# Layer-2 attention scores taken from h W by VectorE inside GraphSAGE's loop, V scaled by one VectorE operation, the projection's pools allotted later

## The chip, the cores and the metric

The kernel runs on one core of one Trainium2 chip. The metric is device time in microseconds (us), the median of several executions. The core has five engines that run side by side and each take their instructions in order: TensorE (PE, with its weight loads shown as PEld), VectorE (DVE), ScalarE (ACT), GpSimd (POOL, which here issues the gathers) and SyncE (SP, which issues the plain DMAs).

## The reference, cut to what matters

Four graph layers run one after another on 3327 nodes with 512 features, and one sparse adjacency matrix serves all of them. Each layer normalises its input, applies a rectifier and adds its result to the input. Layer 0 is graph attention with batch normalisation, layer 1 is GraphSAGE (a mean over the neighbours and two linear maps), and layers 2 and 3 are graph attention with 8 heads of 64 features. The change touches what layer 2's attention needs from its input:

```python
x = x + _L1_gnn_ref(h, adj, ...)
h = jnp.maximum(_layernorm(x, axis=-1), 0.0)
Wh = jnp.einsum('nd,hdo->hno', x, W)
f1 = jnp.einsum('hno,ho->hn', Wh, a1)
f2 = jnp.einsum('hno,ho->hn', Wh, a2)
e = leaky_relu(f1[:, :, None] + f2[:, None, :])
attention = softmax(where(adj > 0, e, NEG_INF))
h_prime = jnp.einsum('hnm,hmo->hno', attention, Wh)
```

The scores f1 and f2 are sums of h W times a1 or a2 over each head's 64 features. They can be had either from h times a narrow matrix (W times a, summed per head, 16 columns), or from h W itself, once that is there.

## The kernel before, in words

All data is fp32. The 3327 nodes are padded to 3328, that is 26 blocks (NB) of 128 rows. The kernel first turns the adjacency matrix into lists of neighbours (`lists`), then tests whether they fit, and runs `sparse`; a dense branch (`general`) exists for other graphs and does not run here. `sparse` goes through these stages in order: attention 0 (`attend`), batch normalisation and layer norm, GraphSAGE, attention 2, attention 3.

**The SAGE loop (from L1472 backwards).** The neighbours of a block lie in up to 37 chunks of 128 gathered rows in the first block and 10 or so in the last ones; there are 359 in all. `load` copies a chunk's mask to fp32 on ScalarE (z_mask, L1453) and gathers its rows of h from HBM through GpSimd (z_rows, L1115, 8 buffers of two chunks). TensorE adds each chunk into sage_acc (L1472). When a block has its last chunk, the generator `ending` takes it on in steps: ScalarE scales it by the degree (s_ag, L1411), TensorE transposes it (a_ps, L1415), ScalarE copies it (aT, L1417), TensorE multiplies by the neighbours' weight (n_ps, L1421), VectorE adds the node's own part y and then the old x (s_o, L1426 and L1427), SP stores it, and `proj.begin` hands the block to the next layer's projection.

**The projection of layer 2 (`Following`) runs inside this loop.** `norm` computes the layer norm's sums on ScalarE (ln_j, L777 and L779), the inverse root partly on VectorE (rs_h, rs_g, rs_y: L713, L715, L719), and the normalised rows ln_h on ScalarE (L788). `rest` then does, for each block: four transposes on TensorE (p_ps, L795); rectifier into hT on ScalarE (L798); the scores p_sd, four fp32 matmuls of hT with the 16 columns of WA (L803, eight records in the profile, since an fp32 matmul is recorded as two); three small ScalarE operations on them (L807, L808, L810); a clip on VectorE (L813); h W into p_wh, four matmuls of 512 columns (L816); exponentials (`halves`, L730 and L731); eight ScalarE operations that scale each head of p_wh into v_row (L820); the store of v_row to the table in HBM (L821); a transpose of the 16 halves (p_tr, L824), its copy r_row (L827) and its store (L829). The four PSUM tiles p_ps, p_sd, p_wh and p_tr take turns in two PSUM banks (pb=2).

**What sets the order.** Every group of chunks calls `tick`, which advances each pending `ending`, each `norm` and up to two `rest` generators by one step, so the generators' `yield`s say where the steps may fall. The loop stands under no written-out order: a scheduling layer that builds the program places the instructions on each engine's in-order queue by their dependences. In the attention stages, the order of TensorE, VectorE and ScalarE is written out by hand; there layer 3's projection runs beside attention 2 with the same class. Attention 2's first gathers need the whole table and so the last block's v_row.

**Memory.** Pools are stacked. The projection's pools (`following`, called with pb=2 before the batch normalisation) lie under those of SAGE, of the batch normalisation (fbn) and of the layer norm (fln), so its weight fWt (L749) can be loaded early. WA for all layers is computed in the first stage by `Products`, which also uses it for a test of range.

Of the kernel before, what the change touches and what calls it, by code (L numbers as in the profile page):

```python
# [23 lines left out]
F32 = mybir.dt.float32  # L24
# [3 lines left out]
I32 = mybir.dt.int32  # L28
# [3 lines left out]
AF = mybir.ActivationFunctionType  # L32
ALU = mybir.AluOpType
ET = mybir.EngineType
AX = mybir.AxisListType
# [3 lines left out]
P = 128  # L39
H = 8  # L40
F = 64
D = H * F
KC = D // P
# [7 lines left out]
GB = 64  # L51
# [5 lines left out]
ROW = H * (F + 1) + H  # L57
# [4 lines left out]
SMALL = 53.0  # L62
# [393 lines left out]
class Products:  # L456
# [4 lines left out]
    def __init__(self, tc, t, pool, wp):  # L461
        self.nc, self.t, self.wp = tc.nc, t, wp
        self.WA = []
        for l in range(3):
            WA = pool.tile([P, KC, 2 * H], F32, name=f"WA{l}")
            self.WA.append(WA)
        self.ok = pool.tile([1, 1], I32, name="ok")
# [234 lines left out]
def rsqrt(nc, pool, cs, v, scale=1.0, bufs=3):  # L702


    n = v.shape[1]
    y = pool.tile([P, n], F32, name="rs_y", tag=f"rs_y{n}", bufs=bufs)
    g = pool.tile([P, n], F32, name="rs_g", tag=f"rs_g{n}", bufs=bufs)
    nc.scalar.activation(g, v, AF.Ln, scale=scale, bias=cs["eps"])
    nc.scalar.activation(y, g, AF.Exp, scale=-0.5)

    def step():
        h = pool.tile([P, n], F32, name="rs_h", tag=f"rs_h{n}", bufs=bufs)
        nc.vector.tensor_scalar(h, v, -0.5 * scale, -0.5 * EPS, ALU.mult, ALU.add)  # L713
        if n == 1:
            nc.vector.tensor_scalar(g, y, y, h, ALU.mult, ALU.mult)  # L715
        else:
            nc.vector.tensor_tensor(g, y, y, ALU.mult)
            nc.vector.tensor_tensor(g, g, h, ALU.mult)
        nc.vector.scalar_tensor_tensor(y, g, 1.5, y, ALU.add, ALU.mult)  # L719
        return y  # L720

    return step


def halves(nc, pool, cs, sf):


    rf = pool.tile([P, H], F32, name="r_full", tag="r_full", bufs=2)
    rs = pool.tile([P, 2, H], F32, name="r_half", tag="r_half", bufs=2)
    nc.scalar.activation(rf, sf, AF.Exp, scale=0.8, bias=cs["down"])  # L730
    nc.scalar.copy(rs.bitcast(F32R)[:, 0, :], rf)  # L731

    def other():
        nc.vector.tensor_tensor(rs.bitcast(F32R)[:, 1, :], rf, rs[:, 0, :], ALU.subtract)
        return rs.rearrange("p t h -> p (t h)")

    return other


class Following:  # L740

    def __init__(self, tc, cs, N, wl, W, WA, table, r_dram, pool, psum, pb=1):
        self.__dict__.update(locals())
        nc = tc.nc
        self.NB = table.shape[0] // P
        self.Wt = pool.tile([P, KC, D], F32, name=f"fWt{wl}")
        nc.sync.dma_start(self.Wt, W.rearrange("(kc p) o -> p kc o", p=P))  # L749
        self.hs = pool.tile([P, self.NB, KC], F32, name=f"hs{wl}")  # L750
        self.early, self.ready = [], []
# [4 lines left out]
    def tick(self):  # L756
        for _ in range(min(2, len(self.ready))):
            while self.ready and next(self.ready[0]) is None:
                self.ready.pop(0)
        for g in list(self.early):  # L760
            hx = next(g)
            if hx is not None:
                self.early.remove(g)
                self.ready.append(self.rest(*hx))

    def drain(self):
        while self.early or self.ready:
# [4 lines left out]
    def norm(self, c, xt):  # L772
        nc, pp, cs = self.tc.nc, self.pool, self.cs

        junk = pp.tile([P, D], F32, name="ln_j", tag="ln_j", bufs=1)
        st = pp.tile([P, 4], F32, name="ln_s", tag="ln_s", bufs=3)
        nc.scalar.activation(junk, xt, AF.Identity, accum_out=st[:, 0:1])  # L777
        nc.scalar.mul(st[:, 1:2], st[:, 0:1], -1.0 / D)
        nc.scalar.activation(junk, xt, AF.Square, bias=st[:, 1:2], accum_out=st[:, 2:3])  # L779
        step = rsqrt(nc, pp, cs, st[:, 2:3], 1.0 / D)  # L780
        yield
        y = step()
        if c == self.NB - 1:
            nc.vector.tensor_tensor(y, y, cs["real"], ALU.mult)
        yield
        hx = pp.tile([P, D], F32, name="ln_h", tag="ln_h", bufs=3)
        nc.scalar.mul(st[:, 3:4], st[:, 1:2], y)
        nc.scalar.activation(hx, xt, AF.Identity, scale=y, bias=st[:, 3:4])  # L788
        yield c, hx

    def rest(self, c, hx):
        nc, pp, WA, wl = self.tc.nc, self.pool, self.WA, self.wl
# [294 lines left out]
def sparse(ctx: ExitStack, tc: tile.TileContext, t: dict, out: bass.AP, WA, ls, cs, idx, rdeg, first):  # L1087
# [5 lines left out]
    nc = tc.nc  # L1093
    N = out.shape[0]
# [5 lines left out]
    def used(c):  # L1100
        return min(P, N - c * P)
# [18 lines left out]
    def attend(layer, table, r_dram, finish, tick=lambda: None, home=None):  # L1120
# [11 lines left out]
        with tc.tile_pool(name=f"fatt{layer}", bufs=2) as ap, tc.tile_pool(  # L1132
# [48 lines left out]
            def later():  # L1181
                for e in list(ends):
                    if next(e, 0) == 0:
                        ends.remove(e)
                tick()
# [60 lines left out]
            while ends:  # L1246
                later()

    def following(lx, layer, wl, W, pb=1):

        table = dram.tile([NP, ROW], I32, name=f"table{layer}")
        r_dram = dram.tile([ls.G, 2, H, GB], F32, name=f"r_dram{layer}")
        pp = lx.enter_context(tc.tile_pool(name=f"fproj{layer}", bufs=1))
        pps = lx.enter_context(tc.tile_pool(name=f"fproj_ps{layer}", bufs=1, space=PSUM))
        return Following(tc, cs, N, wl, W, WA, table, r_dram, pp, pps, pb)

    def elu_into(xin, dst, then=lambda c, xt: None):
        def finish(c, hp, pool):
# [21 lines left out]
    with ExitStack() as mx:  # L1280
# [3 lines left out]
        bias = mid.tile([P, D], F32, name="sage_b")  # L1284
# [56 lines left out]
        Wx = mid.tile([P, 2, KC, D], F32, name="fWx")  # L1341
        nc.sync.dma_start(Wx, wx_dram.rearrange("k kc p o -> p k kc o"))

        proj = following(mx, 2, 1, t["L2_gnn_W"], 2)
        gp = mx.enter_context(tc.tile_pool(name="fsage", bufs=2))
        gps = mx.enter_context(tc.tile_pool(name="fsage_ps", bufs=2, space=PSUM))
        two = [P, 2, D]
        with tc.tile_pool(name="fbn", bufs=1) as bp:
            var_ps = gps.tile([P, D], F32, name="var_ps", tag="n_ps")
            for c in range(0, NB, 2):  # L1350
                d = bp.tile(two, F32, name="bn_d", tag="bn_d", bufs=2)
                nc.vector.tensor_tensor(d, y[:, c : c + 2, :], mean.unsqueeze(1).to_broadcast(two), ALU.subtract)
                nc.scalar.activation(d, d, AF.Square)
                for i in range(2):
                    k = used(c + i)
# [7 lines left out]
        with tc.tile_pool(name="fln", bufs=1) as bp:  # L1363
# [24 lines left out]
            def own(c):  # L1388
                tp = gps.tile([P, KC, P], F32, name="h_ps", tag="a_ps")
                for kc in range(KC):  # L1390
                    nc.tensor.transpose(tp[:, kc, :], y[:, c, kc * P : (kc + 1) * P], cs["ident"])
                hT = bp.tile([P, KC, P], F32, name="hT", tag="hT", bufs=2)
                nc.scalar.copy(hT, tp)  # L1393
                ps = gps.tile([P, D], F32, name="s_ps", tag="n_ps")
                for kc in range(KC):
                    nc.tensor.matmul(ps, hT[:, kc, :], Wx[:, 0, kc, :], start=(kc == 0), stop=(kc == KC - 1))  # L1396
                nc.vector.tensor_tensor(y[:, c, :], ps, bias, ALU.add)
# [6 lines left out]
            for i in range(2):  # L1404
                own(NB - 2 + i)

        ends = []

        def ending(b, acc):
# [51 lines left out]
        for i, (b, _, begins, stops) in enumerate(parts):  # L1461
            load(i + SAHEAD)
            if begins:
                acc = gps.tile([P, D], F32, name="sage_acc", tag="sage_acc")
            at = -1
            for r, u, k, m, z in loaded.pop(i):
                if r != at:
                    at = r
                    tick()
                g = b * PG + u  # L1470
                f, l = k == ls.first[g], k == ls.first[g] + CAPS[g] - 1
                nc.tensor.matmul(acc[u * GB : (u + 1) * GB, :], m, z, start=f, stop=l)  # L1472
            if stops:
                ends.append(ending(b, acc))
        while ends:
            tick()
# [3 lines left out]
    with ExitStack() as l3:  # L1480
        at2 = proj
        proj = following(l3, 3, 2, t["L3_gnn_W"])
        attend(2, at2.table, at2.r_dram, elu_into(x2, x3, proj.begin), proj.tick)
        proj.drain()
# [88 lines left out]
```

## Time and profile before

| What | us |
| --- | --- |
| Median of 3 runs (2575.82, 2585.0, 2585.8) | 2585.0 |
| The profiled execution, its own time | 2951.92 |
| Its span, first to last instruction | 2950.1 |
| Busy: TensorE matmuls / VectorE / ScalarE / GpSimd | 2161.4 / 1781.5 / 1115.7 / 1381.8 |
| Mean granted TensorE clock | 0.791 |

The profiled execution is 14% longer than the median, so times read from it are larger than those of a plain run. A stage is a window of the span. A row of a group reads: line, engine, operation, tile written and tiles read, shape and count, then busy time in us and mean duration of one in ns, then the idle time of the engine just before these instructions and what ended most of it. "issue" is time in which an engine waited for nothing that the profile shows. The ends of matmuls are modelled.

### The profile page before, as it was taken

The page shows a single profiled execution, that of the slowest core. Times are in us where ns is not written, and L with a number is a line of the kernel's source. Part 1 is how long each engine was busy: PE and PEld are TensorE (multiplying, and loading weights), DVE is VectorE, ACT ScalarE, POOL GpSimd, SP SyncE. Part 2 cuts the span into 40 slices and gives each one's busy share as a digit, 9 for nine tenths or more (in the row PEclk, how much of TensorE's full clock was granted, in tenths as well). Part 3 has the DMA queues.
Part 4 walks back from the last instruction along what each step waited for, and adds up shares of the span by engine and source line. Part 5 has one row for each costly group of instructions (what it writes and reads, how often), then busy time and mean ns, then how long its engine had stood idle before and what let it go on. Part 6 is the DMA issues. An engine that isn't in the chain of part 4 may idle for free.

```text
span 2950.1 us, 54237 instructions
## 1 busy us (share of the span) xinstructions
PE 2161.4 (73%) x21320; PEld 1372.2 (47%) x21320; DVE 1781.5 (60%) x2194; ACT 1115.7 (38%) x4044; POOL 1381.8 (47%) x1482
## 2 busy tenths in 40 slices
PE   4777577767775976888998567877777657767775
PEld 2444354555552422233333355655555345556564
DVE  7648587878786800011111377777776277888886
ACT  4543022333434412344455213555666501232333
POOL 1001365666550055665554365555444066666563
PEclk9778688977777997899999777777787766675765
DMA  7761577877662746666665466666565166667774
GB/s 309 282 251 46 174 235 233 252 214 209 201 203 82 246 145 187 189 207 212 198 196 183 133 184 186 200 198 188 178 178 166 45 192 190 193 200 198 201 205 131
DMA packets 188773, 562.09 MB, mean 191 GB/s; under 512 B 37732, under 2 KB 42272, under 8 KB 185182
## 3 DMA queue, kind: packets, MB, share of 16 engines
q0 software_dynamic: 115456, 404.86, 47.2%
q1 hardware_dynamic: 73054, 153.67, 14.7%
q8 instruction: 171, 2.80, 0.4%
q14 instruction: 92, 0.75, 0.1%
HBM read 498.74 MB, written 59.68 MB: 189 GB/s over the span
## 4 chain that ended last, share of the span: by engine, by line
PE 54%; issue 16%; ACT 9%; another core or an unknown queue 3%; DVE 3%; DMA 2%; POOL 1%; SPq 0%; DVEq 0%; ACTq 0%; POOLq 0%
PE facc L1237 28%; PE p_wh L816 7%; PE sage_acc L1472 5%; PE n_ps L1421 3%; PE r_bc L1148 2%; PE p_sd L803 2%; PE s_ps L1396 2%; ACT v_row L820 2%; ACT fhp L1175 1%; PE fwx_ps L1314 1%; PE bmean_ps L1324 1%; PE p_ps L795 1%; ACT hT L798 1%; DMA rows<-table,idx 1%
## 5 line engine op out<-in xcount | busy, mean ns | idle before, releaser
L1115 POOL DMA_INDIRECT rows<-table,idx x1077 | 1023.4, 950 | 873.2 <-PE facc L1237 361.7
L1237 PE MATMUL facc<-rows,wgt 128*64 128x65 f32 x17232 | 975.3, 268 | 412.7 <-issue 394.5
L1237 PEld LDWEIGHTS facc<-rows,wgt 128*64 128x64 f32 x17232 | 826.5, 176 | 628.7 <-issue 576.9
L1223 DVE TENSOR_TENSOR wgt<-mx,mask 128x1536 f32<-128x1536 f32 (+1 forms) x405 | 638.4, 1576 | 158.6 <-PE facc L1237 75.0
L1216 DVE TENSOR_TENSOR mx<-r_bc,rows 128x1536 f32<-128x1536 f32 (+1 forms) x405 | 639.6, 1579 | 144.7 <-PE facc L1237 65.9
L1115 POOL DMA_INDIRECT z_rows<-h_dram,idx x359 | 339.4, 945 | 387.0 <-ACT hT L1393 139.5
L1175 ACT ACTIVATE fhp<-sums,rd 64x64 f32<-64x64 f32 x832 | 219.8, 334 | 137.0 <-DVE rd L1169 71.8
L1472 PE MATMUL sage_acc<-z_rows,z_mask 128*64 128x512 f32 x718 | 225.2, 639 | 9.5 <-DMA z_rows<-h_dram,idx 6.2
L816 PE MATMUL p_wh<-fWt,hT 128*128 128x512 f32 x416 | 227.7, 695 | 1.4 <-ACT s_col L810 1.4
L1165 ACT COPY sums<-facc 128x260 f32<-128x260 f32 x156 | 57.7, 370 | 405.0 <-PE facc L1237 354.3
L813 DVE TENSOR_SCALAR s_col<-s_col 128x8 f32<-128x8 f32 x52 | 9.2, 177 | 306.0 <-issue 135.9
L1208 ACT ACTIVATE mask<-on 128x192 uint8<-128x192 uint16 (+1 forms) x135 | 46.5, 344 | 378.8 <-DVE on L1202 214.1
L816 PEld LDWEIGHTS p_wh<-fWt,hT 128*128 128x128 f32 x416 | 90.3, 228 | 109.8 <-issue 105.3
L820 ACT ACTIVATE v_row<-p_wh,v_row 128x64 f32<-128x64 f32 x416 | 90.4, 328 | 125.8 <-PE p_wh L816 99.3
L1426 DVE TENSOR_TENSOR s_o<-n_ps,bn_y 128x512 f32<-128x512 f32 x26 | 18.0, 691 | 192.2 <-issue 95.6
L1036 POOL DMA_DIRECT2D list_b<-shift x12 | 5.9, 503 | 273.4 <-DVE shift L990 273.4
L680 PE MATMUL wh_ps<-fWt,hT 128*128 128x512 f32 x208 | 128.9, 777 | 0.0
L803 PE MATMUL p_sd<-WA,hT 128*128 128x16 f32 x416 | 74.4, 303 | 70.3 <-ACT hT L798 46.2
L803 PEld LDWEIGHTS p_sd<-WA,hT 128*128 128x128 f32 x416 | 71.8, 246 | 103.9 <-ACT hT L798 59.6
L1175 ACT ACTIVATE bn_y<-sums,rd 64x64 f32<-64x64 f32 x416 | 109.5, 333 | 2.4 <-DVE rd L1169 0.5
L1421 PE MATMUL n_ps<-fWx,aT 128*128 128x512 f32 x208 | 106.1, 646 | 5.6 <-ACT aT L1417 5.5
L1148 PE MATMUL r_bc<-r_two,fones 2*128 2x512 f32 x156 | 95.3, 615 | 14.8 <-issue 8.1
(198 smaller groups left out, 2108.0 us busy)
## 6 DMA issues: line engine op xcount, KB each, us to landing
adj_i<-in_adj SPq DMA_DIRECT2D x26, 1664.0 KB
table<-v_row SPq DMA_DIRECT2D x78, 264.0 KB
rows<-table,idx POOLq DMA_INDIRECT x1077
fin_x<-fx SPq DMA_DIRECT2D x52, 256.0 KB
ln_x<-in_x SPq DMA_DIRECT2D x26, 256.0 KB
bn_x<-in_x SPq DMA_DIRECT2D x13, 512.0 KB
fx<-bn_x SPq DMA_DIRECT2D x13, 512.0 KB
fsage_x<-fx SPq DMA_DIRECT2D x26, 256.0 KB
```

The source lines that it names most:

```text
L680: nc.tensor.matmul(wh, hT[:, kc, :], self.Wt[:, kc, :], start=(kc == 0), stop=(kc == KC - 1))
L803: nc.tensor.matmul(sd[:, : 2 * H], hT[:, kc, :], WA[wl][:, kc, :], start=(kc == 0), stop=(kc == KC - 1))
L816: nc.tensor.matmul(wh, hT[:, kc, :], self.Wt[:, kc, :], start=(kc == 0), stop=(kc == KC - 1))
L820: nc.scalar.mul(V[:, h, 0:F], wh[:, h * F : (h + 1) * F], V[:, h, F : F + 1])
L1115: nc.gpsimd.indirect_dma_start(out=dst, out_offset=None, in_=src[:, :], in_offset=bass.IndirectOffsetOnAxis(ap=idx[:, k : k + 1], axis=0))
L1148: nc.tensor.matmul(rb, ones[0:2, :].bitcast(F32R), rrs.pop(g).bitcast(F32R), start=True, stop=True)
L1175: nc.scalar.mul(hp[o0 : o0 + GB, h * F : (h + 1) * F], sm[mine, q, 0:F], rd[mine, q, :])
L1216: nc.vector.tensor_tensor(mx[:, :n], rbs[g].unsqueeze(1).to_broadcast(full), gt[:, :n, H * (F + 1) : ROW].unsqueeze(3).to_broadcast(full), ...
L1223: nc.vector.tensor_tensor(wt[:, :n], mx[:, :n], mk.unsqueeze(2).to_broadcast(full), ALU.mult)
L1237: nc.tensor.matmul(accs[g][v * GB : (v + 1) * GB, q * (F + 1) : (q + 1) * (F + 1)], wt[:, k, h, :], gt[:, k, h * (F + 1) : (h + 1) * (F + 1)],
L1421: nc.tensor.matmul(ps, aT[:, kc, :], Wx[:, 1, kc, :], start=(kc == 0), stop=(kc == KC - 1))
L1472: nc.tensor.matmul(acc[u * GB : (u + 1) * GB, :], m, z, start=f, stop=l)
```

## The change

`Following` takes an optional pair `ab` of score vectors. Layer 2 gives (a1, a2); layer 3 gives none and keeps `rest`. With `ab`, both vectors are loaded into SBUF, repeated over the partitions, and the new generator `rest_by_rows` takes the place of `rest`. It computes h W first, multiplies it on VectorE by both vectors at once (128 x 1024 products) and sums each head's 64 products (16 sums). The matmuls with WA and the ScalarE copy of the scores go. The eight ScalarE operations that scale V become one VectorE operation. The generator has one `yield` less. The call of `following` for layer 2 moves from before the batch normalisation to after the layer norm's pool is closed, so that its tiles take memory that fbn and fln used.

```diff
-    def __init__(self, tc, cs, N, wl, W, WA, table, r_dram, pool, psum, pb=1):
+    def __init__(self, tc, cs, N, wl, W, WA, table, r_dram, pool, psum, pb=1, ab=None):
         self.__dict__.update(locals())
         nc = tc.nc
+        if ab is not None:
+            self.ab = pool.tile([P, 2, D], F32, name=f"ab{wl}")
+            for k, a in enumerate(ab):
+                nc.sync.dma_start(self.ab[:, k, :], a.partition_broadcast(P))
...
-                self.ready.append(self.rest(*hx))
+                self.ready.append((self.rest if self.ab is None else self.rest_by_rows)(*hx))
...
+    def rest_by_rows(self, c, hx):
+        nc, pp = self.tc.nc, self.pool
+        tp = self.psum.tile([P, KC, P], F32, name="p_ps", tag="p_ps", bufs=self.pb)
+        for kc in range(KC):
+            nc.tensor.transpose(tp[:, kc, :], hx[:, kc * P : (kc + 1) * P], self.cs["ident"])
+        hT = pp.tile([P, KC, P], F32, name="hT", tag="hT", bufs=2)
+        for kc in range(KC):
+            nc.scalar.activation(hT[:, kc, :], tp[:, kc, :], AF.Relu, accum_out=self.hs[:, c, kc : kc + 1])
+        yield True
+        self.mean(c, hT)
+        wh = self.psum.tile([P, D], F32, name="p_wh", tag="p_ps", bufs=self.pb)
+        for kc in range(KC):
+            nc.tensor.matmul(wh, hT[:, kc, :], self.Wt[:, kc, :], start=(kc == 0), stop=(kc == KC - 1))
+        yield True
+        pr = pp.tile([P, 2, D], F32, name="sd_pr", tag="sd_pr", bufs=1)
+        nc.vector.tensor_tensor(pr, wh.unsqueeze(1).to_broadcast([P, 2, D]), self.ab, ALU.mult)
+        sd = pp.tile([P, 2 * H], F32, name="sd_col", tag="sd_col", bufs=2)
+        nc.vector.tensor_reduce(sd, pr.rearrange("p k (h f) -> p (k h) f", f=F), AX.X, ALU.add)
+
+        sf = pp.tile([P, H], F32, name="s_col", tag="s_col", bufs=2)
+        nc.vector.tensor_scalar(sf, sd[:, :H], -SMALL, SMALL, ALU.max, ALU.min)
+        row = pp.tile([P, ROW], F32, name="v_row", tag="v_row", bufs=2)
+        V = row[:, : H * (F + 1)].rearrange("p (h f) -> p h f", f=F + 1)
+        d = sd[:, H : 2 * H]
+        nc.scalar.activation(V[:, :, F : F + 1], d.rearrange("p (h o) -> p h o", o=1), AF.Exp)
+        nc.scalar.activation(row[:, H * (F + 1) :], d, AF.Exp, scale=-0.8, bias=self.cs["down"])
+        rs = halves(nc, pp, self.cs, sf)
+        yield True
+        nc.vector.tensor_tensor(
+            V[:, :, 0:F], wh.rearrange("p (h f) -> p h f", f=F), V[:, :, F : F + 1].to_broadcast([P, H, F]), ALU.mult
+        )
+        nc.sync.dma_start(self.table[c * P : (c + 1) * P, :ROW], row.bitcast(I32))
+        rs = rs()
+        yield True
+        tr = self.psum.tile([2 * H, P], F32, name="p_tr", tag="p_ps", bufs=self.pb)
+        nc.tensor.transpose(tr, rs, self.cs["ident"])
+        rr = pp.tile([2 * H, P], F32, name="r_row", tag="r_row", bufs=2)
+        nc.scalar.copy(rr, tr)
...
+        yield None
...
-    def following(lx, layer, wl, W, pb=1):
+    def following(lx, layer, wl, W, pb=1, ab=None):
...
-        return Following(tc, cs, N, wl, W, WA, table, r_dram, pp, pps, pb)
+        return Following(tc, cs, N, wl, W, WA, table, r_dram, pp, pps, pb, ab)
...
-        proj = following(mx, 2, 1, t["L2_gnn_W"], 2)
         gp = mx.enter_context(tc.tile_pool(name="fsage", bufs=2))
...
                 own(NB - 2 + i)
 
+        proj = following(mx, 2, 1, t["L2_gnn_W"], 2, (t["L2_gnn_a1"], t["L2_gnn_a2"]))
         ends = []
```

More of the change, by code (lines that the diff above doesn't have):

```diff
@@ L789, in norm @@
         yield c, hx
+    def rest_by_rows(self, c, hx):
[35 more added lines that the diff above has]
+        nc.scalar.copy(rr, tr)
+        n = P // GB
+        nc.sync.dma_start(
+            self.r_dram[c * n : (c + 1) * n, :, :, :].rearrange("g t h i -> (t h) g i"),
+            rr.rearrange("h (g i) -> h g i", i=GB),
+        )
+        yield None
```

## The prediction, made before the changed kernel was run

> **What bounds the kernel now.** I read the windows by stage first, since a mean over the whole span mixes stages with different limits. These are GraphSAGE (SAGE below) and its neighbours, then the SAGE loop in three pieces. The columns are length, then busy time (instructions) of PE, PEld, DVE, ACT and POOL, granted clock, DMA share, GB/s.
>
> ```profile
> 1032.00:1665.00 633.00, 517.44 (x1667) 204.28 (x1666) 65.40 (x193) 251.00 (x1054) 337.05 (x357) 0.91 0.59 182
> 1665.00:2355.00 690.00, 507.67 (x6340) 368.08 (x6340) 483.48 (x507) 339.49 (x1326) 336.87 (x356) 0.76 0.59 171
> ...
> 1120.00:1400.00 280.00, 223.94 (x729) 86.41 (x730) 26.77 (x80) 106.67 (x457) 170.29 (x181) 0.90 0.66 202
> 1400.00:1610.00 210.00, 193.19 (x652) 77.78 (x650) 26.81 (x82) 107.97 (x461) 117.21 (x124) 0.96 0.65 199
> 1610.00:1665.00 55.00, 38.29 (x114) 17.14 (x110) 6.29 (x24) 25.20 (x108) 4.23 (x5) 0.81 0.23 76
> ```
>
> In SAGE, TensorE is busy 517 of 633 us and VectorE 65. In the late blocks (1400 to 1610) TensorE reaches 92%. The next stage, attention 2, keeps VectorE busy 483 of 690 us; the new operations don't go there. Next I asked for the chain of waits over 1120 to 1660, to see which work of the projection sets the pace:
>
> ```profile
> by line: PE sage_acc L1472 21.9%; PE n_ps L1421 14.6%; PE p_wh L816 12.6%; another core or an unknown queue 8.7%; issue 7.4%; ACT v_row L820 5.0%; PE p_sd L803 4.8%; PE a_ps L1415 2.6%; PE p_ps L795 2.5%; DMA z_rows<-h_dram,idx 2.4%; ACT ln
> ```
>
> Both steps that the change takes away are on it: the score matmuls (4.8%) and ScalarE's scaling of V (5.0%). The groups of 1120 to 1645 give durations:
>
> ```profile
> L1472 PE MATMUL sage_acc<-z_rows,z_mask 128*64 128x512 f32 x636 | 197.7, 641 | 3.5 <-issue 1.9 <-DMA z_rows<-h_dram,idx 1.5
> ...
> L820 ACT ACTIVATE v_row<-p_wh,v_row 128x64 f32<-128x64 f32 x200 | 43.3, 326 | 30.5 <-PE sage_acc L1472 19.5 <-remote 7.0 <-PE p_wh L816 4.0
> ...
> L803 PE MATMUL p_sd<-WA,hT 128*128 128x16 f32 x200 | 29.5, 265 | 12.1 <-issue 12.1
> L803 PEld LDWEIGHTS p_sd<-WA,hT 128*128 128x128 f32 x200 | 29.2, 203 | 39.8 <-issue 33.1 <-ACT aT L1417 3.2 <-ACT hT L798 3.2
> ...
> L1426 DVE TENSOR_TENSOR s_o<-n_ps,bn_y 128x512 f32<-128x512 f32 x26 | 18.0, 691 | 192.2 <-issue 95.6 <-PE n_ps L1421 55.6 <-PE sage_acc L1472 10.6
> ```
>
> The z gathers could be a second bound. POOL's waits from 1020 to 1670:
>
> ```profile
> POOL z_rows L1115 <- PE sage_acc L1472: 92.8, 34, 8.3
> ...
> POOL z_rows L1115 <- PE p_tr L824: 46.4, 10, 7.3
> ```
>
> POOL waits 139 us for TensorE to give buffers back: TensorE is late, not the gathers. The timeline of TensorE at 1560 shows how ScalarE holds it up:
>
> ```profile
> 1560.38 1.94 PE L1472 MATMUL sage_acc<-z_rows,z_mask 128*64 128x512 f32 x8
> 1565.34 0.44 PE L795 MATMUL p_ps<-fident,ln_h 128*128 128x128 f32 x2 [3.02 <-ACT r_row L827]
> ```
>
> TensorE stands still for 3.02 us until ScalarE, which has just run its eight V scalings (1.73 us), delivers ln_h and r_row.
>
> [...] 128x1024 from PSUM (mx) took 1232 ns, 128x512 (s_o) 691.
>
> **The change, part by part.** All sums are in microseconds of the profiled execution (2951.92, span 2950.1), which is 14% above the median of 2585.0; I convert at the end.
>
> *Score matmuls removed.* 26 blocks of 8 records. Busy time 29.5 in 25 blocks, 1.18 each, so 31 for 26; on the chain 4.8% of 540 is 26. I take -26; bounds -31 and -10 (if much of it only fills waits).
>
> *Eight V scalings and the s_col copy removed from ScalarE.* 8 x 0.33 recorded, 1.74 per block because they overlap: 45 us of ScalarE, and 26 copies of 0.17 add 4. On the chain L820 has 5.0% of 540, 27. Not all comes back: behind it z_mask, s_ag, aT and the layer norm stay on the same in-order engine. What is late next is TensorE itself or the norm's chain. I take two thirds, -18; bounds -27 and 0.
>
> *VectorE's three new operations.* The product over 2 x 512 from PSUM: 1.23 (the mx row). The sum over 1024 elements to 16: a 512-element reduce (L481) took 0.69; a further 512 at the 0.53 to 0.54 by which 1024 exceeds 512 above gives 1.22. V scaled in one operation: 0.69 (L636 does just this in the first projection). Together 3.14, times 26: 82 on an engine idle for 568 of 633. As work it is hidden. As latency it isn't by itself: p_tr (and so the PSUM bank) needs product, sum, clip (0.17), exp (0.30), cast (0.20) and subtraction (0.17) after the last p_wh matmul, 3.3, some 3.9 with hand-overs of 0.1. In the built program's order, most late blocks have eight sage_acc matmuls and three transposes between p_wh and p_tr: 8 x 0.485 plus 0.4 is 4.3; most middle blocks have n_ps (3.43) and one to three sage_acc instead. The cover is thin. Behind the waiting product on VectorE stand rs_g and rs_y of the next norm, for which ln_h and then p_ps wait. I take +5; bounds 0 and +82, if every block waits in full.
>
> *Projection allotted later.* Its DMAs (fWt, 1 MB) leave SP's place at 900 us, ahead of bn_x, where it was issued 40 us before the next load; nothing waited for it. They now stand behind the last h_dram store and wait for the layer norm's pool, free when the last s_ps product has been added, about 1075; with the two 256 KB broadcasts 1.5 MB, 5 us at the 309 GB/s that the fastest slice of the profile page shows, beside the first gathers. SP's next instruction is the store of s_o at 1125, and p_wh first needs the weights at 1132, so the wait itself holds up nothing. I take +2; bounds 0 and +8 if the first gathers queue behind it. POOL's own order is unchanged. Cover lost: if it landed after 1132, each late us costs one.
>
> *End of the stage.* For the last block, product, sum, exps (0.4) and V (0.69) with hand-overs, about 3.8, replace score matmuls (1.0) and scalings (1.74) ahead of the table's store, on which attention 2's gathers wait: +1; bounds 0 and +2.
>
> *Unchanged.* WA of layer 2 is still computed for the range test; layer 3 keeps the old rest.
>
> Sum: -26 - 18 + 5 + 2 + 1 = -36, 1.2%; scaled by 2585/2952 (0.876), -31.5, so about 2553.
>
> **Rivals.**
> *The wait moves to VectorE (slower).* Product, sum and scaling stand between p_wh and p_tr in every block, with two PSUM banks for p_ps, p_wh and p_tr, and TensorE in order behind p_tr. For it: the cover is only 0.4 us too long, and rs_g stands behind the product. Against: VectorE is otherwise nearly idle, and p_sd no longer takes a bank. Price: 26 x 3.14 = 82, less the 53 removed at most, plus 29; times 0.876, +25: 2610. It decides once TensorE waits over 2.0 us per block (53/26).
> *Gathers take over (no change).* In the first 14 blocks (up to 37 gathers at 1.25 us) TensorE's freed time would become waiting for z_rows; for it is 2.4% of the chain in z_rows, against it POOL's 139 us. Then 12 blocks of 26 gain: -36 x 12/26 = -17, times 0.876: 2570; with a thin VectorE wait besides, 2580.
> *ScalarE was the true pacer (larger gain).* Both chain terms in full, -53, [...]: -65, times 0.876: 2528.
> *It doesn't do what it says.* In the built program p_sd is gone from SAGE alone and nothing before it moves but the weight load; I give this no chance of its own.
>
> **How the numbers follow.** Forecast 0.57 (2540 to 2570), larger gain 0.08, no change 0.17, slower 0.18. About 0.5% (13 us) is what a measurement of this kernel tells from no change: faster is 0.66 (forecast, larger gain, a little of the no-change case), same 0.16, slower 0.18. The range 2522 to 2600 takes in the larger gain and the no-change case, and half-paid VectorE waits, and leaves out most of the slower one.
>
> **What would show it.** SAGE, 1032 to 1665, should take about 597 us in the profile after, TensorE's busy time there down by some 30, ScalarE's by 45 or more, VectorE's up by 82. The new product should show 1.2 us. Right if POOL's waits for sage_acc shrink; wrong if p_tr or p_ps waits for VectorE or for r_half more than 2 us per block, or if idle time before sage_acc goes to z_rows.

## The result and the profile after

| | us |
| --- | --- |
| Before, median of 4 runs | 2583.64 |
| After, median of 4 runs (2553.76 to 2558.84) | 2557.27 |
| Ratio after to before | 0.9919, 95% interval 0.9901 to 0.9937 |
| After, profiled execution: its own time / span / clock | 2553.76 / 2551.8 / 0.851 |

The change made the kernel faster by 0.8% (0.6% to 1.0%), which is 21 us (16 to 26); the two medians stand 26 us apart. The profile after has a span close to its median, whereas the profile of before that the prediction worked from had 2950. A second profile of the kernel before, `e0_before_again`, has a span of 2576.2, and it is the one that the profile after is compared with below.

The stages by window, from the first sage_acc matmul to the first gather of attention 2, and from there to the end; columns as in the prediction. First before (`e0_before_again`):

```profile
941.00:1470.00 529.00, 495.32 (x1666) 195.28 (x1664) 66.20 (x194) 254.73 (x1054) 334.10 (x353) 0.98 0.71 216
1470.00:2576.00 1106.00, 741.94 (x12138) 596.90 (x12138) 942.95 (x881) 498.24 (x1846) 685.57 (x718) 0.77 0.71 209
```

Then the changed kernel:

```profile
937.00:1448.00 511.00, 460.62 (x1463) 168.24 (x1461) 141.92 (x272) 209.30 (x820) 335.64 (x355) 0.98 0.74 229
1448.00:2552.00 1104.00, 729.23 (x12136) 584.41 (x12136) 943.23 (x881) 498.18 (x1846) 686.10 (x718) 0.79 0.71 208
```

The gain lies in SAGE: 529 became 511, and the stages around it differ by 2 to 4 us. TensorE's busy time in SAGE fell by 34.7, ScalarE's by 45.4, and VectorE's rose by 75.7. TensorE lost 35 us of work and the stage became only 18 shorter, so half of what was freed turned into idle time. Two stretches of the loop fare differently: from the first p_ps transpose of block 0 to that of block 10 (blocks count from 0), and from there to that of block 25. Before:

```profile
1021.10:1228.10 207.00, 192.81 (x656) 73.26 (x655) 23.23 (x70) 100.54 (x417) 156.68 (x166) 0.99 0.80 247
1228.10:1453.80 225.70, 222.75 (x784) 92.16 (x783) 34.61 (x106) 134.91 (x571) 129.15 (x137) 1.00 0.70 216
```

After:

```profile
1017.50:1227.60 210.10, 189.96 (x590) 64.41 (x590) 53.87 (x100) 84.27 (x331) 159.22 (x168) 0.99 0.80 247
1227.60:1432.20 204.60, 191.92 (x651) 74.86 (x649) 76.29 (x151) 107.18 (x431) 127.54 (x135) 0.99 0.75 235
```

The whole gain lies in the later stretch, where TensorE was busy for 99% of the time before: 226 became 205. In the first ten blocks nothing was gained (207 and 210). The chain of waits over the loop and the stage's end, before:

```profile
by line: PE sage_acc L1472 31.4%; PE n_ps L1421 18.4%; PE p_wh L816 17.9%; DMA z_rows<-h_dram,idx 12.7%; PE p_sd L803 4.6%; PE p_ps L795 3.2%; PE a_ps L1415 2.9%; POOL z_rows L1115 1.5%; issue 1.4%; ACT v_row L820 1.0%; PE p_tr L824 0.9%; A
```

After:

```profile
by line: PE sage_acc L1522 24.8%; PE n_ps L1471 17.7%; PE p_wh L808 17.2%; DMA z_rows<-h_dram,idx 17.1%; issue 5.2%; POOL z_rows L1165 4.6%; PE p_ps L800 3.1%; PE a_ps L1465 1.8%; DVE v_row L824 1.3%; PE p_tr L831 1.0%; DVE sd_col L813 0.8%
```

p_sd (4.6%) is gone, the gathers' share (z_rows by DMA and by POOL) went from 14% to 22%, and sage_acc itself shrank from 31% to 25%, though its matmuls are the same. ScalarE's scaling of V was 1.0% of the chain before, not the 5.0% of the first profile. Two rows of the groups before, with ScalarE's and TensorE's removed work:

```profile
L820 ACT ACTIVATE v_row<-p_wh,v_row 128x64 f32<-128x64 f32 x208 | 45.0, 326 | 26.2 <-PE p_wh L816 26.2
L803 PE MATMUL p_sd<-WA,hT 128*128 128x16 f32 x208 | 29.4, 259 | 1.9 <-DVE hT L699 1.9
```

What took its place, in the changed kernel:

```profile
L811 DVE TENSOR_TENSOR sd_pr<-p_wh,ab 128x1024 f32<-128x1024 f32 x26 | 31.8, 1225 | 141.4 <-PE p_wh L808 141.4
L813 DVE TENSOR_REDUCE sd_col<-sd_pr 128x16 f32<-128x1024 f32 x26 | 31.6, 1214 | 0.4
L824 DVE TENSOR_TENSOR v_row<-p_wh,v_row 128x512 f32<-128x512 f32 x26 | 18.0, 691 | 11.5 <-ACT v_row L820 10.6
```

The three durations are what the prediction took (1.23, 1.22, 0.69). The timeline shows a late block, from one group of p_ps transposes to the next. Before, TensorE has no idle time left:

```profile
1384.81 1.08 PE L1472 MATMUL sage_acc<-z_rows,z_mask 128*64 128x512 f32 x4
1385.81 3.70 PE L1421 MATMUL n_ps<-fWx,aT 128*128 128x512 f32 x8
1389.35 0.96 PE L803 MATMUL p_sd<-WA,hT 128*128 128x16 f32 x8
1390.24 1.08 PE L1472 MATMUL sage_acc<-z_rows,z_mask 128*64 128x512 f32 x4
1391.25 3.70 PE L816 MATMUL p_wh<-fWt,hT 128*128 128x512 f32 x8
...
1398.99 1.07 PE L1472 MATMUL sage_acc<-z_rows,z_mask 128*64 128x512 f32 x2
1399.99 0.28 PE L803 MATMUL p_sd<-WA,hT 128*128 128x16 f32 x1
```

After:

```profile
1380.28 0.66 PE L800 MATMUL p_ps<-fident,ln_h 128*128 128x128 f32 x4
1380.77 3.60 PE L1471 MATMUL n_ps<-fWx,aT 128*128 128x512 f32 x8
1384.21 3.60 PE L808 MATMUL p_wh<-fWt,hT 128*128 128x512 f32 x8
1387.73 3.65 PE L1522 MATMUL sage_acc<-z_rows,z_mask 128*64 128x512 f32 x16
1391.32 0.55 PE L1465 MATMUL a_ps<-fident,s_ag 128*128 128x128 f32 x3
1392.45 0.28 PE L831 MATMUL p_tr<-fident,r_half 128*16 128x128 f32 x1 [0.58 <-DVE r_half L734]
1392.56 0.27 PE L1465 MATMUL a_ps<-fident,s_ag 128*128 128x128 f32 x1
1392.76 1.08 PE L1522 MATMUL sage_acc<-z_rows,z_mask 128*64 128x512 f32 x4
1393.77 0.66 PE L800 MATMUL p_ps<-fident,ln_h 128*128 128x128 f32 x4
```

A late block now takes 13.5 us; before, two took 29.2 together (14.2 and 15.0). p_tr does wait for VectorE's chain, 0.58 us: the cover is as thin as the prediction said. Over the stage p_tr waits 11.4 us for VectorE, 7.4 of it in the last two blocks, and sage_acc's matmuls wait 33 us for z_rows where they waited 23 before: both have a part in the new idle time.

The two profiles also show why sage_acc shrank. Two records are one chunk; before, the chunk at 1398.99 stands alone among score matmuls and takes 1.00 us until the next instruction starts, while the four records at 1392.76, two chunks, take 1.01. A chunk's records have the form 128*64, those of p_wh 128*128, and the kernel adds the two chunks of a pair into different halves of sage_acc's rows. Where they follow each other, their first records start 0.007 us apart, so the two ran side by side. Counted over the whole loop, 38 of the 359 chunks stood alone between other matmuls before and 16 after: by these durations that makes an estimated 22 x 0.5 = 11 us of TensorE that no part of the diff names. In the order that the scheduling layer had built, the score matmuls and the transposes parted pairs; how the change made it build another order was not followed up.

### The profile page after: what moved, and what is told of

Its sections match the earlier page's. It is cut to its first block, busy times and chain, and to the rows that moved or that the text cites. A ratio compares the mean times of both kernels' runs of the same rounds, so it can differ in the third digit from the quotient of the medians.

```text
span 2551.8 us, 53690 instructions
## 1 busy us (share of the span) xinstructions
PE 1825.0 (72%) x21112; PEld 1161.8 (46%) x21112; DVE 1852.3 (73%) x2272; ACT 1068.3 (42%) x3810; POOL 1387.4 (54%) x1482
## 4 chain that ended last, share of the span: by engine, by line
PE 30%; DVE 24%; issue 13%; ACT 9%; DMA 8%; POOL 3%; DVEq 0%; SPq 0%; POOLq 0%; ACTq 0%
DVE mx L1266 12%; PE facc L1287 8%; DVE wgt L1273 8%; PE sage_acc L1522 4%; DMA z_rows<-h_dram,idx 4%; PE p_wh L866 4%; DMA rows<-table,idx 3%; PE n_ps L1471 3%; PE p_wh L808 3%; ACT fhp L1225 2%; POOL z_rows L1165 2%; PE s_ps L1445 2%; POOL rows L1165 1%; ACT bn_y L1225 1%; ACT v_row L870 1%
## 5 line engine op out<-in xcount | busy, mean ns | idle before, releaser
L1287 PE MATMUL facc<-rows,wgt 128*64 128x65 f32 x17232 | 722.5, 253 | 393.7 <-DVE wgt L1273 259.7
L1287 PEld LDWEIGHTS facc<-rows,wgt 128*64 128x64 f32 x17232 | 667.1, 165 | 518.2 <-DVE wgt L1273 310.5
L1522 PE MATMUL sage_acc<-z_rows,z_mask 128*64 128x512 f32 x718 | 209.8, 618 | 33.0 <-DMA z_rows<-h_dram,idx 32.6
L811 DVE TENSOR_TENSOR sd_pr<-p_wh,ab 128x1024 f32<-128x1024 f32 x26 | 31.8, 1225 | 141.4 <-PE p_wh L808 141.4
L1522 PEld LDWEIGHTS sage_acc<-z_rows,z_mask 128*64 128x64 f32 x718 | 52.2, 137 | 156.2 <-issue 77.6
L866 PE MATMUL p_wh<-fWt,hT 128*128 128x512 f32 x208 | 117.2, 714 | 1.4 <-ACT s_col L860 1.4
L1503 ACT CAST z_mask<-mask 128x128 f32<-128x128 uint8 (+1 forms) x196 | 52.7, 284 | 118.7 <-PE sage_acc L1522 117.5
L1471 PE MATMUL n_ps<-fWx,aT 128*128 128x512 f32 x208 | 98.7, 608 | 0.0
L808 PE MATMUL p_wh<-fWt,hT 128*128 128x512 f32 x208 | 96.9, 610 | 2.0 <-DVE hT L699 1.9
L1445 PE MATMUL s_ps<-fWx,hT 128*128 128x512 f32 x208 | 93.5, 603 | 3.4 <-ACT hT L1442 3.4
L1198 PE MATMUL r_bc<-r_two,fones 2*128 2x512 f32 x156 | 89.1, 575 | 6.6 <-DMA r_two<-r_dram 3.6
```

Source lines behind the costliest of these rows:

```text
L808: nc.tensor.matmul(wh, hT[:, kc, :], self.Wt[:, kc, :], start=(kc == 0), stop=(kc == KC - 1))
L866: nc.tensor.matmul(wh, hT[:, kc, :], self.Wt[:, kc, :], start=(kc == 0), stop=(kc == KC - 1))
L1198: nc.tensor.matmul(rb, ones[0:2, :].bitcast(F32R), rrs.pop(g).bitcast(F32R), start=True, stop=True)
L1287: nc.tensor.matmul(accs[g][v * GB : (v + 1) * GB, q * (F + 1) : (q + 1) * (F + 1)], wt[:, k, h, :], gt[:, k, h * (F + 1) : (h + 1) * (F + 1)],
L1471: nc.tensor.matmul(ps, aT[:, kc, :], Wx[:, 1, kc, :], start=(kc == 0), stop=(kc == KC - 1))
```

## The experiments

Theory A: before the change TensorE paces the late blocks and the gathers already pace the early ones; the change makes TensorE lighter, and the gathers take over and swallow a part. Rival B: the gathers paced the loop already, so the gain comes from elsewhere. Rival C: TensorE paces everything before and after. Rival D, from the prediction: VectorE's chain becomes the wait. The ratios below are to the kernel before measured beside each of them, and a gain in us is worked out from the ratio unless it says otherwise.

**The kernel before, profiled again** (`e0_before_again`, no edit). 

> The kernel before, unchanged, profiled once more, because its first profile had a span of 2950 us where plain runs take 2584. Expected of both theories: a span near 2582 us. Theory A (TensorE and ScalarE pace SAGE's loop before the change, the gathers after it): the SAGE stage, from the first sage_acc to the first gather of attention 2, takes 535 to 545 us here (513 in the profile after, plus the 26 gained), TensorE's idle time before sage_acc is put down to z_rows for under 60 us (101 after), and POOL waits for sage_acc and p_tr over 100 us (40 after). Rival B (the gathers already pace the loop before, and the gain lies elsewhere): SAGE within 10 us of 513, and z_rows waits of about 100 us.

Measured 2578.0 us, span 2576.2, SAGE 529: short of A's 535 to 545, and above the 523 that B allows. TensorE's waits for z_rows before sage_acc (its weight loads and matmuls) were 63 us (101 after), as A expects within a few. POOL's waits fell short of A's 100. In the kernel before:

```profile
POOL z_rows L1115 <- PE sage_acc L1472: 37.5, 48, 6.8
POOL z_rows L1115 <- PE p_tr L824: 23.4, 8, 4.8
```

In the changed kernel:

```profile
POOL z_rows L1165 <- issue: 68.9, 226, 0.3
...
POOL z_rows L1165 <- PE sage_acc L1522: 40.4, 55, 6.8
```

61 us became 40, all of it by p_tr; the waits for sage_acc did not shrink. A gather took POOL 0.95 us by the mean, and 0.30 more passed before the next where POOL waited for nothing (68.9 over 226): 1.25, so 359 need 449. They ran from 933.7 to 1426.4 before (493) and from 930.1 to 1403.6 after (474). After, that is 25 us above this floor, and before 44, which speaks against both C and B but settles neither; half of p_wh and half of the gathers, below, do.

**The scores alone** (`e1_scores_alone`): the changed kernel with ScalarE's scaling put back.

```diff
-        nc.vector.tensor_tensor(
-            V[:, :, 0:F], wh.rearrange("p (h f) -> p h f", f=F), V[:, :, F : F + 1].to_broadcast([P, H, F]), ALU.mult
-        )
+        for h in range(H):
+            nc.scalar.mul(V[:, h, 0:F], wh[:, h * F : (h + 1) * F], V[:, h, F : F + 1])
```

> Scores from h W by VectorE and the late allotment, but V scaled by ScalarE's eight operations as before. By the prediction's terms: -26 + 4 + 2, scaled, about -17: 2566 us. Theory A (the gathers take over once either of the two is lighter, so the parts don't add up): -18 to -26, that is nearly the whole gain alone. Rival (V's scaling is what pays): 0 to -8.

Measured 2566.8 us, 0.996 (0.9947 to 0.9973): -10 us (-7 to -14), short of the prediction's -17 and of A's range, and touching the rival's 0 to -8. Its loop, first to last sage_acc, took 487 us (500 before, 480 after), but the end of the stage grew from 29 to 37. Its last two blocks, TensorE:

```profile
1445.17 0.28 PE L830 MATMUL p_tr<-fident,r_half 128*16 128x128 f32 x1 [3.74 <-DVE r_half L734]
1447.54 1.11 PE L800 MATMUL p_ps<-fident,ln_h 128*128 128x128 f32 x4 [2.09 <-ACT ln_h L793]
1450.55 6.43 PE L808 MATMUL p_wh<-fWt,hT 128*128 128x512 f32 x8 [1.90 <-DVE hT L699]
1460.66 0.38 PE L830 MATMUL p_tr<-fident,r_half 128*16 128x128 f32 x1 [3.68 <-DVE r_half L734]
```

Where no gather work is left to cover it, the chain over VectorE costs 3.7 us per block, and ln_h then stands behind the eight scalings on ScalarE (2.09).

**V's scaling alone** (`e2_v_alone`): in the kernel before, layer 2 only (pb is 2 there).

```diff
+        if self.pb == 2:
+            nc.vector.tensor_tensor(
+                V[:, :, 0:F], wh.rearrange("p (h f) -> p h f", f=F), V[:, :, F : F + 1].to_broadcast([P, H, F]), ALU.mult
+            )
+        else:
+            for h in range(H):
+                nc.scalar.mul(V[:, h, 0:F], wh[:, h * F : (h + 1) * F], V[:, h, F : F + 1])
```

> Only layer 2's V scaled by one VectorE operation; the scores stay on TensorE and the allotment early. By the prediction's terms: -18 + 1, scaled, about -15: 2569 us. Theory A (parts that don't add up): -12 to -26. Rival (TensorE's removed matmuls are what pays, ScalarE is off the path in a plain run): 0 to -6.

Measured 2560.84 us, 0.9935 (0.9922 to 0.9948): -17 us (-13 to -20), inside A's range and close to the term. Of the two parts this one pays more. Its SAGE stage:

```profile
941.00:1459.00 518.00, 486.12 (x1664) 192.32 (x1662) 83.01 (x219) 215.39 (x846) 334.25 (x353) 0.98 0.72 221
```

Set against 529 before, 11 us are gone, 9 of them TensorE's busy time, though its instructions are the same. The order explains much of it. In blocks 10 to 15, where TensorE has no idle time with either kernel, 14 chunks stood alone before and none does here. The start of such a block before (17 us long, 12 chunks):

```profile
1228.64 1.07 PE L1472 MATMUL sage_acc<-z_rows,z_mask 128*64 128x512 f32 x2
1229.64 0.66 PE L1415 MATMUL a_ps<-fident,s_ag 128*128 128x128 f32 x4
1230.13 0.29 PE L803 MATMUL p_sd<-WA,hT 128*128 128x16 f32 x2
1230.36 1.07 PE L1472 MATMUL sage_acc<-z_rows,z_mask 128*64 128x512 f32 x2
1231.36 0.84 PE L803 MATMUL p_sd<-WA,hT 128*128 128x16 f32 x6
1232.13 1.07 PE L1472 MATMUL sage_acc<-z_rows,z_mask 128*64 128x512 f32 x2
```

And with V alone (15 us long, 12 chunks too):

```profile
1228.02 1.08 PE L1477 MATMUL sage_acc<-z_rows,z_mask 128*64 128x512 f32 x4
1229.03 0.66 PE L1420 MATMUL a_ps<-fident,s_ag 128*128 128x128 f32 x4
1229.53 0.96 PE L803 MATMUL p_sd<-WA,hT 128*128 128x16 f32 x8
1230.42 1.08 PE L1477 MATMUL sage_acc<-z_rows,z_mask 128*64 128x512 f32 x4
```

That makes these five blocks 7.5 us shorter: TensorE gets the same work done sooner, and no wait for ScalarE is taken away. The stage's end is 2.7 us shorter. The 7 us that blocks 0 to 5 gain, of which a later start of block 0 takes 3 back, I could not assign. Starting times of p_ps show where each kernel gains (us between the projections of the named blocks):

| blocks | before again | V alone | a quarter of the scores | after |
| --- | --- | --- | --- | --- |
| 0 to 5 | 127.1 | 119.7 | 123.9 | 122.5 |
| 5 to 10 | 79.9 | 84.2 | 82.5 | 87.6 |
| 10 to 15 | 82.2 | 74.8 | 74.5 | 72.6 |
| 15 to 25 | 143.5 | 142.8 | 141.1 | 132.0 |

Every kernel that gains ahead gives some of it back in blocks 5 to 10. In blocks 15 to 25 V's scaling alone pays nothing.

**The late allotment alone** (`e3_late_alone`): the kernel before, with one line moved.

```diff
-        proj = following(mx, 2, 1, t["L2_gnn_W"], 2)
...
                 own(NB - 2 + i)
 
+        proj = following(mx, 2, 1, t["L2_gnn_W"], 2)
         ends = []
```

> Only the call of following for layer 2 moved behind the layer norm. By the prediction's term +2: 2585 us, within 0 to +7. Rival (the weight's load out of the batch normalisation's way, or other memory under SAGE's pools, is worth something): -3 to -10.

Measured 2576.03 us, 0.9996 (0.9985 to 1.0007), -4 to +2 us: nothing measurable. The +2 can't be told from zero, and of the rival's gain all beyond 4 us is excluded.

**A quarter of the score matmuls** (`e5_quarter_scores`): TensorE's side of the change with nothing added to VectorE.

```diff
-        for kc in range(KC):
-            nc.tensor.matmul(sd[:, : 2 * H], hT[:, kc, :], WA[wl][:, kc, :], start=(kc == 0), stop=(kc == KC - 1))
+        ks = 1 if self.pb == 2 else KC
+        for kc in range(ks):
+            nc.tensor.matmul(sd[:, : 2 * H], hT[:, kc, :], WA[wl][:, kc, :], start=(kc == 0), stop=(kc == ks - 1))
```

> The kernel before with one of the four score matmuls per block in SAGE; three quarters of the score sums are left out. It takes TensorE's cost away without giving VectorE anything. By the prediction's term, three quarters of -26, scaled: -17, so 2561 us. Theory A (GpSimd issues a gather every 1.25 us, 449 us for 359, and already sets the pace of the early blocks; TensorE paces only the late ones): -5 to -12, 2566 to 2573 us. Rival (TensorE paces all blocks): -17 to -25.

Measured 2562.9 us, 0.9942 (0.9921 to 0.9963): -15 us (-9 to -20), between the two theories' ranges and touching both. TensorE's busy time in SAGE:

```profile
941.00:1457.00 516.00, 477.90 (x1513) 176.60 (x1511) 66.26 (x194) 251.60 (x1054) 335.96 (x354) 0.98 0.72 222
```

17 us less than before, for a stage 13 shorter. For all four matmuls the same rate gives -20 (-13 to -27).

**The product twice** (`e6_product_twice`): the changed kernel, 2.44 us more of VectorE ahead of p_tr in every block.

```diff
-        nc.vector.tensor_tensor(pr, wh.unsqueeze(1).to_broadcast([P, 2, D]), self.ab, ALU.mult)
         sd = pp.tile([P, 2 * H], F32, name="sd_col", tag="sd_col", bufs=2)
-        nc.vector.tensor_reduce(sd, pr.rearrange("p k (h f) -> p (k h) f", f=F), AX.X, ALU.add)
+        for _ in range(2):
+            nc.vector.tensor_tensor(pr, wh.unsqueeze(1).to_broadcast([P, 2, D]), self.ab, ALU.mult)
+            nc.vector.tensor_reduce(sd, pr.rearrange("p k (h f) -> p (k h) f", f=F), AX.X, ALU.add)
```

> The changed kernel with VectorE's product and sum run twice in a row, 2.44 us more per block on VectorE and ahead of p_tr. The slower rival of the prediction (no cover left): +40 to +56 against the changed kernel's 2557, so about 2600 to 2613 us. Theory A (about a third of a microsecond is covered in most blocks, and where the loop waits for gathers anyway the latency is hidden too): +5 to +25, 2562 to 2582 us. Fully hidden: 2557 to 2560 us, the last block's tail alone.

Measured 2558.0 us, 0.9924 (0.9895 to 0.9953) against 0.9919: of the 63 us added to VectorE, 1 us shows, give or take 9. That excludes the +40 to +56 and most of A's +5 to +25. TensorE's wait for VectorE at p_tr, which was 11.4 in the changed kernel, is here:

```profile
L832 PE MATMUL p_tr<-fident,r_half 128*16 128x128 f32 x26 | 7.4, 286 | 12.3 <-DVE r_half L734 12.3
```

Rival D falls as what paces the loop. The order is built again for each kernel, and p_tr moves further from p_wh when its inputs take longer: from the start of the last p_wh record to p_tr the median is 2.4 us before, 5.2 after and 8.1 here. The end of the stage, where nothing can be put between, grew from 30 to 35 us; the loop in this one profile was as much shorter. Its order also leaves only 5 chunks alone, against 16, which is worth 5 us by the figure above, so a cost of that size may be hidden in the result.

**Half of p_wh** (`e7_half_wh`): the changed kernel without two of the four p_wh matmuls, 1.7 us per block less for TensorE, 45 in all.

```diff
-        for kc in range(KC):
-            nc.tensor.matmul(wh, hT[:, kc, :], self.Wt[:, kc, :], start=(kc == 0), stop=(kc == KC - 1))
+        for kc in range(2):
+            nc.tensor.matmul(wh, hT[:, kc, :], self.Wt[:, kc, :], start=(kc == 0), stop=(kc == 1))
```

> The changed kernel with two of the four p_wh matmuls per block in SAGE; half of h W's sum for layer 2 is left out. TensorE gets 1.7 us lighter per block, 45 us in all. Theory A (POOL's issue is the next bound: gathers ran 474 us after the change where 449 are the floor): -10 to -25, 2532 to 2547 us, with POOL's waits for sage_acc nearly gone. Rival (TensorE still paces the loop): -40 to -45, about 2515 us.

Measured 2542.35 us, 0.9868 (0.9837 to 0.9898): -15 us against the changed kernel by the medians and -13 by the ratios, give or take 9, as A expects and a third of what was taken off. TensorE's busy time in SAGE fell by 28 only (461 to 433): sage_acc's, with the same matmuls, rose from 210 to 226 us. POOL's waits for sage_acc fell from 40 to 29 us, where A expected them nearly gone. The chain of waits in its loop:

```profile
by line: DMA z_rows<-h_dram,idx 37.9%; PE sage_acc L1522 18.6%; PE n_ps L1471 11.8%; POOL z_rows L1165 8.4%; issue 8.2%; PE p_wh L808 7.3%; PE p_ps L800 2.5%; PE a_ps L1465 1.0%; DVE v_row L824 0.7%; DVE sd_pr L811 0.6%; DVE sd_col L813 0.6
```

The gathers hold 46% of it, TensorE 41%. All of the gain lies in blocks 10 to 25 (205 became 192); the first ten took 211 us, as after the change (210). There TensorE does not pace the loop, which rules out C.

**Gathers further ahead** (`e8_gathers_ahead`): the changed kernel with `SROWS = 10` and `SAHEAD = 3` for 8 and 2.

> The changed kernel with ten z_rows buffers in place of eight and three groups loaded ahead in place of two. Theory A: the gathers can run ahead in the late blocks and POOL waits less for buffers (40 us of waits for sage_acc after the change), but the early blocks stay at one gather per 1.25 us: 0 to -12, 2545 to 2557 us. Rival (the waits for z_rows are DMA time, not issue): no change, within 4 us of 2557.

Measured 2554.14 us, 0.9905 (0.9883 to 0.9927). It lies 3 us ahead of the changed kernel by the medians, inside both intervals: not settled. POOL's waits for sage_acc fell from 40 to 25 us. It is the best whole kernel of this study, but not clearly better than the changed one.

**Half of the gathers** (196 of the 359 stay), in the changed kernel (`e9_half_gathers`) and in the kernel before (`e10_before_half_gathers`), then both again (`e11_half_gathers_again`, `e12_before_half_gathers_again`).

```diff
-                        gather(zt[:, k, :], h_dram, k0 + k)
-                        zs.append((k, u, k0 + k, mf[:, k, :], zt[:, k, :]))
+                        if k == 0:
+                            gather(zt[:, k, :], h_dram, k0 + k)
+                        zs.append((k, u, k0 + k, mf[:, k, :], zt[:, 0, :]))
```

> The changed kernel with one gather for each pair of chunks in SAGE, both chunks' matmuls reading the same rows: about half of the 359 gathers are left out, all matmuls stay. Theory A (POOL's issue is the floor after the change): TensorE paces the loop, which gets 20 to 40 us shorter: 2517 to 2537 us, with idle time before sage_acc for z_rows near zero. Rival (the gathers are covered): 0 to -6.

> The kernel before with the same half of the gathers left out. Theory A (the gathers swallowed a part of the change's gain): with the gathers out of the way, the changed kernel stands 28 to 40 us ahead of the one before, not 21 to 26; this one then takes 2550 to 2572 us. Rival (the gathers took nothing from the gain): the distance stays at 21 to 26 us.

> The changed kernel with one gather for each pair of chunks in SAGE, once more: the call before landed on a chip on which the kernel before takes 2947 us, so that the two halved kernels could be compared with each other (32 us apart) but not with the changed kernel. On a chip where the kernel before takes about 2580: Theory A (POOL's issue is the floor after the change): 2517 to 2537 us. Rival: 2551 to 2557.

> The kernel before with the same half of the gathers left out, once more. Theory A: 28 to 40 us behind its changed counterpart, against 21 with all gathers. Rival: 21 to 26.

The kernel before, measured beside them, took 2946.91 us the first time and 2979.85 the second, so the times expected can't be held against these. The two halved kernels took 2787.08 and 2818.85, 0.9446 (0.9406 to 0.9486) and 0.9553 (0.9515 to 0.959), and the second time 2799.79 and 2837.26, 0.9404 (0.9378 to 0.943) and 0.9507 (0.9485 to 0.9529). By the medians they stand 32 and 37 us apart, inside A's 28 to 40, with the changed part ahead; by the ratios both times 31, with intervals that reach down into the rival's 21 to 26. SAGE of the halved changed kernel:

```profile
1038.00:1498.00 460.00, 435.47 (x1459) 164.59 (x1458) 141.36 (x271) 207.58 (x820) 180.31 (x190) 0.99 0.52 162
```

And of the halved kernel before:

```profile
1034.00:1527.00 493.00, 474.50 (x1672) 193.46 (x1670) 66.20 (x194) 252.82 (x1054) 180.71 (x191) 0.99 0.47 146
```

With the gathers out of the way TensorE is busy for 95% and 96% of the stage, its work differs by 39 us (29 of scores and 11 of pairs make 40), and the stage by 33. With all gathers it was 35 and 18. The changed kernel with all its gathers was not measured beside these, so how much it would gain there stays open, and the two totals alone don't show that the gathers took the difference. The starting times of p_ps do (us):

| blocks | before again | before, half of the gathers | after | after, half of the gathers | after, half of p_wh |
| --- | --- | --- | --- | --- | --- |
| 0 to 10 | 207.0 | 181.3 | 210.1 | 174.2 | 210.7 |
| 10 to 25 | 225.8 | 225.8 | 204.6 | 202.3 | 191.8 |

In blocks 10 to 25 the gathers hardly matter: with half of them the time is the same, before and after, and what TensorE has to do decides. In blocks 0 to 10 the gathers decide: leaving half out takes 26 and 36 us, although the whole kernel took longer there, and lighter work for TensorE takes nothing. The change gains there only with half of the gathers gone (181 to 174; the second time 191 to 175). That is Theory A; B, with gathers that pace the loop throughout, falls.

## Why the prediction was right, point by point

The forecast was 2553, -31.5 us; measured were 2557.27, -26 by the medians and -21 by the ratio (-16 to -26). The forecast case is the one that came, at a lower size. That the total came so near is in part luck: the sum lacked 11 us that TensorE gained from its order, and about 17 us that were freed and not paid out.

*Score matmuls, -26 in the profile, -23 scaled.* Right for taking them away: they were 29.4 us of TensorE, and a quarter left in place gives -20 (-13 to -27) for all four. Handing them to VectorE without the second part paid only -10, with a stage's end that was 8 us longer. The step missed the pairs of chunks that were parted. Of the four matmuls' eight records, one follows another after 0.11 us by the median in both profiles of before.

*V scalings, -18, -16 scaled.* The size came out right (-17 alone), the mechanism did not, so the fit is luck. The prediction read from the first profile that ScalarE holds TensorE up, 5.0% of the chain and a stall of 3.02 us. In the second profile that share is 1.0%, and TensorE waits for nothing in blocks 10 to 25; the stall belonged to the first profile. What V alone gains in the loop is in good part TensorE's order (14 lone chunks gone from blocks 10 to 15, 7.5 us); 2.7 us are the stage's end, and the gain in blocks 0 to 5 is unexplained. The rival with a larger gain (2528) counts 12 us beyond the two terms of the chain (-53); no run shows these 12.

*VectorE's operations, +5.* About right for this order: p_tr waits 0.58 us in seven late blocks, 4 us in the loop, and the durations were right to 0.01 us. From the product's start to the end of r_half 4.0 us passed by the median of the 26 blocks, where the prediction counted 3.9 from the end of p_wh. It is a price of the order and not of the work, since with twice the product the order changed and these late waits went away.

*Late allotment, +2.* No effect found (-4 to +2). In the changed kernel the weight's DMA was issued at 973 us, and the first store of s_o, next on SP, at 1006.

*End of the stage, +1.* Right: 28.8 became 29.8.

*What the sum lacked.* The terms were added as if every block paid. Of the 26 blocks the first ten pay nothing, since the gathers pace them. That was the rival "gathers take over". It was given its place rightly (the early blocks) but as an alternative to the forecast; it happened inside it, and one of the prediction's own signs of being wrong came with it: TensorE's waits for z_rows grew from 63 to 101 us, and POOL's waits for sage_acc, which were to shrink, went from 37.5 to 40.4. The argument against it, POOL's 139 us of waits, came from the first profile; the second has 61. The parts measured alone make -0.40% (scores with the late allotment) and -0.65%, together -1.05%, against -0.8% for all in one; that difference lies within their intervals.

The scaling by 0.876 was a guess that the shape of the stage stays when the whole is 14% longer. It does not: SAGE in the first profile, 629 us by the same measure, was 19% longer than 529, and its waits were others. The chain that the prediction read had 8.7% on "another core or an unknown queue", in pieces of up to 7.8 us, which it left without a term; the chain of the second profile has none. The clock had no part in the gain: granted were 0.98 in SAGE before and after.

## What to carry to other kernels

Before pricing a change, hold the profiled execution's time against the median; where they differ by 14%, the shares of a chain, and above all its stalls, may not be those of a plain run, while durations of single instructions came out nearly alike here (a V scaling 326 ns in both profiles of before, a record of the score matmuls 265 and 259). When an engine that paces a stage is made lighter, ask block by block what else sets the pace (here a gather every 1.25 us in the first ten blocks) and count the gain only where nothing else does. The score matmuls cost more than their own time where they parted two chunks that otherwise ran side by side (1.00 us for one alone, 1.01 for two): count such places in the order. And where the order is built anew for each kernel, a change on one engine can pay through the order on another (V's scaling taken from ScalarE: 7.5 us on TensorE in blocks 10 to 15).

## What the runs showed of the hardware

One 128*64 fp32 chunk of 512 columns that stood alone took 1.00 us on TensorE until the next instruction, and a pair of them 1.01 (medians of 16 and 28 in the changed kernel). Where POOL had no buffer to wait for, gathers were issued every 1.25 us (median before, after and with the product twice), with VectorE busy for 66, 142 and 203 us of the stage. The unchanged kernel took 2575 to 2584 us in some measurements and 2947 to 2980 in others, as long as in the first profile of before; one chip number, 6, stands in the record beside medians of both kinds, so that chips differ is not shown. The DMA rate in attention 0 (400 to 800 us) was 259 GB/s in the second profile of before, 224 in the first and 223 in the halved one. Blocks 10 to 25 took 257.9 us in the first profile and 225.8 in the second, but also 225.8 in the halved kernel before, whose span was 2818: the added time there went with the gathers and not with TensorE's work. What sets it off was not tried.
